# Layer 3 of a four-layer cross-attention kernel: hand order on four engines, exponentials after the pieces, value sums multiplied from PSUM

## The chip, the cores and the metric

The kernel runs on one core of a Trainium2 chip, in float32 throughout. The metric is the device time of one execution in microseconds; the time before is the median of three runs, 3840.64 us (3837.99 to 3846.04). A core has five instruction streams that matter here: TensorE (PE, with its weight loads as PEld), VectorE (DVE), ScalarE (ACT), GpSimd (POOL) and SyncE (SP), which issues the transfers. Each takes its own instructions in order, and waits for another only where a buffer or a value demands it.

## What is computed

Four layers follow each other on a tensor of 4 batches x 512 rows x 512 columns: a grouped-query attention (layer 0), two RWKV recurrences (layers 1 and 2), and a perceiver-style attention with an MLP (layer 3). Only layer 3 is touched:

```python
h = jnp.concatenate([x, latents], axis=1)             # x: context, latents: result of layer 2
q = (latents @ q_w + q_b).reshape(b, k_len, NH, DH)   # 16 heads of 32
kv = (h @ kv_w + kv_b).reshape(b, p + k_len, NH, DH, 2)
kmat, v = (kv[..., 0], kv[..., 1])
attn = jnp.einsum('bkhd,bnhd->bhkn', q, kmat) / DH    # 512 queries, 1024 keys
attn = softmax(where(full_mask, attn, -inf))
attn_out = jnp.einsum('bhkn,bnhd->bkhd', attn, v).reshape(b, k_len, H)
attn_out = attn_out @ out_w + out_b + residual
out = rmsnorm(attn_out, postnorm_w)
out = gelu(out @ mlp_w1 + mlp_b1) @ mlp_w2 + mlp_b2 + residual
```

## The kernel before, in words

Layer 3 splits its work into 16 **units**, a batch `b` times a slice `m` of 128 columns (4 heads of 32), numbered 0 to 15 here. The 1024 keys are 8 blocks of 128. A loop over **steps** (`for i in range(NU + NB + LAG)`, L1358) runs three units at once, each at a different stage, eight steps to a unit:

- `least(u, lt, a)` (L1179) for the newest unit: four score matmuls into `psc`, one for each head, and four VectorE operations (L1189) that keep the running minimum in `mx` (the scores are negated).
- `turned(old, s)` for the unit before: four transposed score matmuls into `pst` (L1175), four VectorE subtractions of the minimum `mb` (L1220) into the tile `aT`, then one ScalarE exponential over all 2048 columns (L1223 for the four masked context blocks, L1225 for the others), and on GpSimd a sum over the blocks into `acc` (L1228 once, L1230 six times). `spread` at s = 0 makes `mb` from `mx` (matmuls `pb`, ScalarE copies L1211).
- `values` two steps behind that (`LAG = 2`): four matmuls into `po` (L1235), which accumulates over eight blocks.

A unit closes in the step in which `ws` is 7, which is step s = 1 of the unit after it: `counted` (L1254) multiplies `acc` with ones into `pn` (L1235) and takes the reciprocal `rs` (L1261); `values` adds the last block and copies `po` into `y` on ScalarE (L1252); `divided` (L1263) multiplies `y` by `rs` (L1267).

Between these stand **pieces**, generators that yield after each bite of matmul work. `early` is the preparation of the next unit: `prep` makes `q`, keys (`pk`) and values (`pv`), and ahead of a new batch `begin` (L1113) loads context and mask (`mi` to `nm` L1121, `mci` to `mc` L1126) and transposes the residual (`ptx`). `rest` is the finish of the last complete batch: `finish` (L1269) multiplies by the output weights (`pout`), adds bias and residual (L1280, L1281), squares and sums on ScalarE (L1284), scales and takes the power -1/2 (`rms`, DVE L78, POOL L79), multiplies (L1286), adds `b2` to the residual on GpSimd (L1287), transposes (`ptn`, L1300), then runs the MLP: `ph` matmuls with a gelu eviction into `hT` (L1320), and `po` (here called `po2` after its code) with an addition into `x` (L1329). A step has a slot for a piece after `least` and one more after `turned`. `behind(i)` says how many of the 38 finish pieces should still be left at step i.

The pools matter: one PSUM pool of seven buffers (tag `s`) is handed round in order of allocation to `psc`, `pst`, `pb`, `pn` and the pieces; `po` has one buffer of its own; `aT` has three, `acc` and `mb` one each.

**What sets the order.** Layers 0 to 2 are inside `tc.manual_schedule` for PE, DVE, ACT and POOL: the instructions stand as written. Layer 3 is inside `tc.manual_schedule(engines={E.PE})`: TensorE's stand as written, and a scheduler decides those of the other engines (L1409).

```python
                if old:
                    turned(old, s)
                if left > min(34, behind(i)) and piece(rest):
                    left -= 1
                if 0 <= w < len(units):
                    values(units[w], ws)
                    if ws == NB - 1:
                        divided(units[w])
```

Of the kernel before, what the change touches and what calls it, by code (L numbers as in the profile page):

```python
# [8 lines left out]
F32 = mybir.dt.float32  # L9
I32 = mybir.dt.int32  # L10
AF = mybir.ActivationFunctionType
ALU = mybir.AluOpType
# [3 lines left out]
P = 128  # L16
B, L, C = 4, 512, 512
KC = C // P
# [12 lines left out]
def tile_xattn_rwkv_perceiver(ctx: ExitStack, tc: tile.TileContext, t: dict, out: bass.AP):  # L31
    nc = tc.nc
# [1054 lines left out]
    def layer3():  # L1087
        NH, HD, N = 16, 32, 2 * L
        NB = N // P
        NR = 4  # L1090
        T2 = 2 * P
        with (
# [18 lines left out]
            st = [{} for _ in range(B)]  # L1111
# [24 lines left out]
            def prep(b, m):  # L1136

                d = st[b]
                ms = slice(m * P, (m + 1) * P)
                w3 = {}  # L1140
                for x in "qkv":
                    w3[x] = bp.tile([P, KC, P], F32, tag="w3" + x, name="w3" + x)
                    nc.sync.dma_start(w3[x], t["L3_W" + x][:, ms].rearrange("(k p) n -> p k n", p=P))
                q = d["q", m] = bp.tile([P, L], F32, tag="q", name="q", bufs=3)
                pm = ps_s.tile([P, L], F32, tag="s", name="pq")
                mm(pm, [(w3["q"][:, k, :], d["xT"][:, k, :]) for k in range(KC)])
                nc.scalar.activation(q, pm, AF.Identity, bias=cols[:, m, 0:1], scale=-1.0 / HD)
                yield
                kT = d["k", m] = bp.tile([P, 2, L], F32, tag="kT", name="kT", bufs=3)
                v = d["v", m] = bp.tile([P, NB, P], F32, tag="v", name="v", bufs=3)  # L1150
                for a, src in enumerate((d["cT"], d["xT"])):
                    pm = ps_s.tile([P, L], F32, tag="s", name="pk")
                    mm(pm, [(w3["k"][:, k, :], src[:, k, :]) for k in range(KC)])
                    nc.scalar.activation(kT[:, a, :], pm, AF.Identity, bias=cols[:, m, 1:2])
                    yield
                    pm = ps_s.tile([P, LT, P], F32, tag="s", name="pv")
                    for j in range(LT):
                        mm(pm[:, j, :], [(src[:, k, j * P : (j + 1) * P], w3["v"][:, k, :]) for k in range(KC)])
                    nc.vector.tensor_tensor(
                        v[:, a * LT : (a + 1) * LT, :],  # L1160
                        pm,
                        vb[:, None, ms].to_broadcast([P, LT, P]),
                        ALU.add,
                    )
                    yield
# [3 lines left out]
            def row_scores(lhsT, rhs, name):  # L1169

                ps = []
                for r in range(NR):
                    rs = slice(32 * r, 32 * r + 32)
                    psc = ps_s.tile([P, L], F32, tag="s", name=name)
                    nc.tensor.matmul(psc, lhsT[rs], rhs[rs], start=True, stop=True, tile_position=(32 * r, 0))  # L1175
                    ps.append(psc)
                return ps
# [35 lines left out]
            def turned(u, s):  # L1213

                b, m = u
                d = st[b]
                ps = row_scores(d["k", m][:, s // LT, s % LT * P : (s % LT + 1) * P], d["q", m], "pst")
                w = d["w", s] = sp.tile([P, NR, L], F32, tag="aT", name="aT", bufs=3)
                for r in range(NR):
                    nc.vector.tensor_tensor(w[:, r, :], ps[r], d["mb"][:, r, :], ALU.subtract)  # L1220
                wf = w.rearrange("p r l -> p (r l)")
                if s < LT:
                    nc.scalar.activation(wf, wf, AF.Exp, bias=d["mc"][:, s : s + 1], scale=-1.0)  # L1223
                else:
                    nc.scalar.activation(wf, wf, AF.Exp, scale=-1.0)  # L1225
                if s == 1:
                    acc = d["acc", m] = sp.tile([P, NR, L], F32, tag="acc", name="acc", bufs=1)
                    nc.gpsimd.tensor_tensor(acc, d["w", 0], w, ALU.add)  # L1228
                elif s > 1:
                    nc.gpsimd.tensor_tensor(d["acc", m], d["acc", m], w, ALU.add)  # L1230

            def columns(po, lhsT, rhs, **kw):

                for r in range(NR):
                    nc.tensor.matmul(  # L1235
                        po[32 * r : 32 * r + 32, :], lhsT(r), rhs[:, r, :], tile_position=(0, 32 * r), **kw
                    )

            def values(u, s):

                b, m = u
                d = st[b]
                if s == 0:
                    d["po"] = ps_o.tile([P, L], F32, tag="o", name="po")
                v = d["v", m]
                columns(
                    d["po"], lambda r: v[:, s, 32 * r : 32 * r + 32], d["w", s], start=(s == 0), stop=(s == NB - 1)
                )
                if s == NB - 1:
                    if "y" not in d:  # L1250
                        d["y"] = bp.tile([P, KC, L], F32, tag="y", name="y")
                    nc.scalar.copy(d["y"][:, m, :], d["po"])  # L1252

            def counted(u):  # L1254

                b, m = u
                d = st[b]
                pn = ps_s.tile([P, L], F32, tag="s", name="pn")
                columns(pn, lambda r: ones, d["acc", m], start=True, stop=True)
                rs = d["rs", m] = sp.tile([P, L], F32, tag="sc", name="rs")  # L1260
                nc.vector.reciprocal(rs, pn)  # L1261

            def divided(u):  # L1263
                b, m = u
                d = st[b]
                y = d["y"][:, m, :]
                nc.vector.tensor_tensor(y, y, d["rs", m], ALU.mult)  # L1267

            def finish(b):  # L1269

# [63 lines left out]
            def chain(*gens):  # L1334
                for x in gens:
                    yield from x

            def piece(*gens):
                return any(next(x, NB) is None for x in gens)
# [4 lines left out]
            units = [(b, m) for b in range(B) for m in range(KC)]  # L1344
            NU = NB * len(units)

            def behind(i):

                if i < NU - NB * (KC - 1) + 2:
                    return 38 * ((1 - i) % (NB * KC)) // (NB * KC)  # L1350
                return sum(0.75 if j < NU - NB else 1.35 if j < NU else 2 for j in range(i + 1, NU + NB))
# [6 lines left out]
            for i in range(NU + NB + LAG):  # L1358
                n, s = divmod(i, NB)
                u, old = [units[j] if 0 <= j < len(units) else None for j in (n, n - 1)]  # L1360
                if u and s == 0:
                    for _ in early:
                        pass
                    b, m = u
                    if m + 1 < KC:
                        early = prep(b, m + 1)
                    elif b + 1 < B:
                        early = chain(begin(b + 1), prep(b + 1, 0))
                w, ws = divmod(i - NB - LAG, NB)
                if u and ws == 0 and w and w % KC == 0:  # L1370
                    for _ in rest:
                        pass
                    rest = finish(w // KC - 1)
                    left = 38
                if u:
                    least(u, s // 2, s % 2)
                if piece(early):
                    pass
                elif piece(rest):
                    left -= 1  # L1380
                if old:
                    if s == 0:
                        spread(old)
                if ws == NB - 1 and 0 <= w < len(units):
                    counted(units[w])
                if old:
                    turned(old, s)
                if left > min(34, behind(i)) and piece(rest):
                    left -= 1
                if 0 <= w < len(units):  # L1390
                    values(units[w], ws)
                    if ws == NB - 1:
                        divided(units[w])
# [5 lines left out]
    E = mybir.EngineType  # L1399
    with (  # L1400
# [5 lines left out]
        layer0(ahead, ep)  # L1406
        for _ in ahead:
            pass
    with tc.manual_schedule(engines={E.PE}):  # L1409
        layer3()  # L1410


# [62 lines left out]
```

## Time and profile before

| | |
|---|---|
| median of the three runs | 3840.64 us |
| profiled execution: its own time / its span | 3843.51 us / 3841.5 us |
| layers 0 to 2 | to about 2420 us of the span |
| layer 3, steps with full flow | about 2480 to 3700 us |
| layer 3, last finish | about 3700 us to the end |
| busy, share of the span: PE / DVE / ACT / POOL | 93% / 72% / 44% / 46% |
| granted TensorE clock, mean | 0.965 |

In the profile, times in a timeline row are the start in the span and the duration, both in us; in groups, busy us and mean ns of one. A bracket at a row's end is the idle time of its engine just ahead of it, with the instruction that ended it. An x8 row of `psc`, `pst`, `po` or `pn` is four matmuls (each has two records).

### The profile page before, as it was taken

How to read it: one execution, taken by the hardware profiler on the slowest of the kernel's cores; microseconds unless marked ns; L12 is line 12 of the kernel's file. 1: busy time of each engine (PE TensorE's matmuls, PEld its weight loads, DVE VectorE, ACT ScalarE, POOL GpSimd, SP SyncE). 2: the span in 40 equal slices, each digit the busy share in tenths (PEclk: the TensorE clock that was granted, in tenths of full speed). 3: DMA queues.
4: the chain of work that ended last, by engine and by line, in shares of the span. 5: the costliest groups of instructions: out<-in, count | busy, mean ns of one | idle time of the engine just before them, and what ended most of it. 6: DMA issues, size and time to landing. Idle time of an engine off the chain costs nothing.

```text
span 3841.5 us, 52407 instructions
## 1 busy us (share of the span) xinstructions
PE 3589.6 (93%) x20544; PEld 1900.9 (49%) x20544; DVE 2765.4 (72%) x4665; ACT 1691.6 (44%) x2514; POOL 1768.4 (46%) x834
## 2 busy tenths in 40 slices
PE   9999999988899999999999967899999999999989
PEld 3333333455565665655665634444454444544446
DVE  6777777689988888888888871388655665667531
ACT  4777676533444444444444422133343334324531
POOL 4777777424444444444444432065533433444430
PEclk9999999989999999999999988899999999999999
DMA  4000000166677777777777754200022122121223
GB/s 149 23 12 23 12 9 20 51 143 133 146 168 176 180 182 171 178 172 167 170 170 171 176 126 129 69 28 17 31 90 70 58 65 71 59 67 36 91 93 121
DMA packets 188805, 386.66 MB, mean 101 GB/s; under 512 B 18128, under 2 KB 44880, under 8 KB 186512
## 3 DMA queue, kind: packets, MB, share of 16 engines
q1 hardware_dynamic: 150256, 251.72, 20.8%
q0 software_dynamic: 38304, 131.61, 18.5%
q8 instruction: 162, 2.65, 0.3%
q14 instruction: 83, 0.68, 0.1%
HBM read 247.50 MB, written 4.19 MB: 66 GB/s over the span
## 4 chain that ended last, share of the span: by engine, by line
PE 64%; DVE 15%; DMA 6%; issue 5%; POOL 5%; ACT 5%; SPq 0%; POOLq 0%; DVEq 0%; ACTq 0%
PE pm L73 9%; PE pv L73 6%; PE po L73 5%; DMA kv<-A 5%; PE ph L73 5%; PE psc L242 5%; PE pst L279 4%; PE pst L1175 3%; PE psc L1175 3%; PE po L304 3%; PE pr L73 3%; DVE ry L867 3%; PE pk L73 3%; PE po L1235 2%; DVE kv L862 2%
## 5 line engine op out<-in xcount | busy, mean ns | idle before, releaser
L1230 POOL TENSOR_TENSOR acc<-acc,aT 128x2048 f32<-128x2048 f32 x96 | 435.0, 4531 | 420.4 <-ACT aT L1225 235.6
L292 POOL TENSOR_TENSOR aT<-aT,nmT 128x1536 f32<-128x1536 f32 x124 | 428.6, 3461 | 206.8 <-ACT aT L290 183.4
L254 DVE CUSTOM_DVE_ANT_0 sc<-psc,nm 128x512 f32<-128x512 f32 x512 | 354.0, 691 | 147.0 <-PE psc L242 89.3
L1220 DVE TENSOR_TENSOR aT<-pst,mb 128x512 f32<-128x512 f32 x512 | 317.4, 681 | 132.0 <-PE pst L1175 132.0
L867 DVE TENSOR_TENSOR ry<-kv,o_r 128x1024 f32<-128x1024 f32 x256 | 347.7, 1398 | 3.5
L862 DVE TENSOR_TENSOR_SCAN kv<-W,kv 128x1032 f32<-128x1032 f32 x128 | 296.1, 2313 | 0.2 <-DMA kv<-A 0.2
L584 POOL DMA_DIRECT2D kv<-A x127 | 118.9, 936 | 379.9 <-DVE kv L839 376.8
L290 ACT COPY aT<-pst 128x512 f32<-128x512 f32 x372 | 196.4, 595 | 178.2 <-PE pst L279 177.7
L298 ACT ACTIVATE aT<-aT 128x2048 f32<-128x2048 f32 x128 | 246.7, 1929 | 5.7 <-POOL aT L292 4.9
L73 PE MATMUL po<-l_m,hT 128*128 128x512 f32 x512 | 237.0, 606 | 9.2 <-ACT hT L1320 9.0
L73 PE MATMUL ph<-nT,l_m 128*128 128x256 f32 x1024 | 240.7, 391 | 0.0
L73 PEld LDWEIGHTS ph<-nT,l_m 128*128 128x128 f32 x1024 | 195.1, 194 | 64.9 <-issue 27.2
L1228 POOL TENSOR_TENSOR acc<-aT 128x2048 f32<-128x2048 f32 x16 | 72.4, 4524 | 327.6 <-ACT aT L1223 327.6
L833 DVE TENSOR_TENSOR A<-vr,o_k 128x1024 f32<-128x1024 f32 x128 | 155.6, 1216 | 88.1 <-DMA kv<-A 88.0
L279 PE MATMUL pst<-q,km 32*128 32x512 f32 x1024 | 206.2, 639 | 9.4 <-DVE mxs L254 5.8
L1189 DVE CUSTOM_DVE_ANT_0 sc<-psc,zeros,mx 128x512 f32<-128x512 f32 x256 | 177.5, 746 | 50.7 <-PE psc L1175 48.4
L1225 ACT ACTIVATE aT<-aT 128x2048 f32<-128x2048 f32 x64 | 122.3, 1911 | 196.6 <-DVE aT L1220 191.6
L1223 ACT ACTIVATE aT<-aT,mc 128x2048 f32<-128x2048 f32 x64 | 128.2, 2003 | 180.3 <-DVE aT L1220 171.0
L242 PE MATMUL psc<-km,q 32*128 32x512 f32 x1024 | 198.8, 653 | 0.8 <-ACT q L223 0.8
L881 PE MATMUL py<-ry,k 128*32 128x512 f32 x1024 | 158.5, 626 | 42.4 <-DVE ry L867 29.6
L929 POOL TENSOR_TENSOR gn_rs<-gn_rs,mhalf 128x64 f32<-128x64 f32 x16 | 186.4, 11648 | 23.0 <-DVE gn_rs L927 23.0
L1189 DVE CUSTOM_DVE_ANT_0 sc<-psc,nm 128x512 f32<-128x512 f32 x256 | 162.9, 686 | 46.5 <-PE psc L1175 45.0
(266 smaller groups left out, 7189.9 us busy)
## 6 DMA issues: line engine op xcount, KB each, us to landing
l_m<-in_L_W SPq DMA_DIRECT2D x64, 1024.0 KB, 5.1
kv<-A POOLq DMA_DIRECT2D x127, 516.0 KB, 7.4
L_wk<-in_L_Wk SPq DMA_DIRECT2D x16, 1024.0 KB, 8.0
L_wr<-in_L_Wr SPq DMA_DIRECT2D x16, 1024.0 KB, 7.8
L_wv<-in_L_Wv SPq DMA_DIRECT2D x16, 1024.0 KB, 6.0
L_wg<-in_L_Wg SPq DMA_DIRECT2D x16, 1024.0 KB, 7.8
L_wo<-in_L_Wo SPq DMA_DIRECT2D x64, 256.0 KB, 7.5
L_fk<-in_L_fWk SPq DMA_DIRECT2D x16, 1024.0 KB, 8.3
```

The lines of the kernel that those rows point to most:

```text
L73: nc.tensor.matmul(ps, lhsT, rhs, start=(i == 0), stop=(i == len(pairs) - 1))
L242: nc.tensor.matmul(psc, d["q"][g][rs, lt * P : (lt + 1) * P], d["km"][rs, a, :], start=True, stop=True, tile_position=(32 * r, 0),)
L254: nc.vector.tensor_tensor_reduce(sc, ps[r], d["nm"][lt], 1.0, -3.0e38, ALU.add, ALU.max, mxs[:, a, lt, c : c + 1])
L279: nc.tensor.matmul(pst, d["km"][rs, a, s * P : (s + 1) * P], d["q2", a][rs, :], start=True, stop=True, tile_position=(32 * r, 0),)
L292: nc.gpsimd.tensor_tensor(w[:, n:, :], w[:, n:, :], nmT[:, None, :].to_broadcast([P, NR - n, L]), ALU.add)
L298: nc.scalar.activation(w, w, AF.Exp)
L862: nc.vector.tensor_tensor_scan(flat(kv), flat(W[g % 2]), flat(kv), 0.0, ALU.mult, ALU.add)
L867: nc.vector.tensor_tensor(y, kv[:, 4 * h : 4 * h + 4, None, :TP].to_broadcast([P, 4, 2, TP]), d["r"][:, i].rearrange("p (o m) -> p o m", o ...
L1175: nc.tensor.matmul(psc, lhsT[rs], rhs[rs], start=True, stop=True, tile_position=(32 * r, 0))
L1189: nc.vector.tensor_tensor_reduce(sc, ps[r], d["nm"][a], 1.0, mx[:, 0, lt, r : r + 1] if a else 3.0e38, ALU.add, ALU.min, mx[:, a, lt, r : ...
L1220: nc.vector.tensor_tensor(w[:, r, :], ps[r], d["mb"][:, r, :], ALU.subtract)
L1230: nc.gpsimd.tensor_tensor(d["acc", m], d["acc", m], w, ALU.add)
```

## The change

Four things, all in layer 3:

1. The whole of layer 3 is in `manual_schedule` for all four engines, so DVE, ACT and POOL too take their instructions as written.
2. The exponential and the sum into `acc` leave `turned` and become `weights(old, s)`, called after the second piece slot.
3. The reciprocal leaves `counted` and becomes `inverted`, called after `turned`; the matmuls into `pn` stay where they are.
4. ScalarE's copy of `po` is gone; `divided` multiplies `po` in PSUM by `rs` into `y`.

```diff
-                if s == NB - 1:
-                    if "y" not in d:
-                        d["y"] = bp.tile([P, KC, L], F32, tag="y", name="y")
-                    nc.scalar.copy(d["y"][:, m, :], d["po"])
...
+            def inverted(u):
+                d = st[u[0]]
+                rs = d["rs"] = sp.tile([P, L], F32, tag="sc", name="rs")
+                nc.vector.reciprocal(rs, d["pn"])
...
             def divided(u):
                 b, m = u
                 d = st[b]
-                y = d["y"][:, m, :]
-                nc.vector.tensor_tensor(y, y, d["rs", m], ALU.mult)
+                if "y" not in d:
+                    d["y"] = bp.tile([P, KC, L], F32, tag="y", name="y")
+                nc.vector.tensor_tensor(d["y"][:, m, :], d["po"], d["rs"], ALU.mult)
...
                 if old:
                     turned(old, s)
+                if ws == NB - 1 and 0 <= w < len(units):
+                    inverted(units[w])
                 if left > min(34, behind(i)) and piece(rest):
                     left -= 1
+                if old:
+                    weights(old, s)
...
-    with tc.manual_schedule(engines={E.PE}):
+    with tc.manual_schedule(engines={E.PE, E.DVE, E.Activation, E.Pool}):
         layer3()
```

Set side by side, the built orders of the two kernels differ in this and in nothing else:

- TensorE: not at all. Layers 0 to 2: not at all.
- VectorE: the reciprocal (16 times) stands after the four subtractions instead of ahead of them, and `y` right behind it, or behind one `x` addition. In each `finish` the scale of `rms` and the multiplication of `ao` stand right behind the addition of the residual; before, one minimum lay ahead of the first and another between the two. `mc` stands beside `nm` instead of up to a unit ahead.
- ScalarE: the 16 copies of `po` are gone. Gelu evictions and squares stand ahead of the exponential of their step instead of behind it. The table loads between gelu and exponential fall from 86 to 74 in the program.
- GpSimd: the power of `rms` stands ahead of that step's sum into `acc` and of the addition of `b2`; before, both lay ahead of it.
- SyncE: three loads of `mci` stand behind their batch's `mi` instead of at the start of the layer.

More of the change, by code (lines that the diff above doesn't have):

```diff
@@ L1220, in turned, with weights @@
                     nc.vector.tensor_tensor(w[:, r, :], ps[r], d["mb"][:, r, :], ALU.subtract)
+            def weights(u, s):
+                b, m = u
+                d = st[b]
+                w = d["w", s]
                 wf = w.rearrange("p r l -> p (r l)")
@@ L1257, in counted @@
                 d = st[b]
-                pn = ps_s.tile([P, L], F32, tag="s", name="pn")
+                pn = d["pn"] = ps_s.tile([P, L], F32, tag="s", name="pn")
                 columns(pn, lambda r: ones, d["acc", m], start=True, stop=True)
-                rs = d["rs", m] = sp.tile([P, L], F32, tag="sc", name="rs")
-                nc.vector.reciprocal(rs, pn)
+            def inverted(u):
+                d = st[u[0]]
+                rs = d["rs"] = sp.tile([P, L], F32, tag="sc", name="rs")
+                nc.vector.reciprocal(rs, d["pn"])
             def divided(u):
```

## The prediction

> **What bounds the kernel now.** First the table of windows, layer 3 by stretch (us; busy of PE, PEld, DVE, ACT, POOL with counts; granted clock; DMA): steps of batch 0, its finish up to the transposes, the long flow after, the last unit.
>
> ```profile
> 2546.00:2710.00 164.00, 162.27 (x932) 72.29 (x928) 137.03 (x303) 62.66 (x52) 95.29 (x21) 1.00 0.08 23
> 2710.00:2770.00 60.00, 52.31 (x259) 25.46 (x256) 41.81 (x92) 14.10 (x16) 29.80 (x13) 0.97 0.09 27
> 2770.00:3060.00 290.00, 285.95 (x1435) 141.36 (x1433) 178.05 (x361) 119.19 (x120) 108.68 (x24) 0.99 0.22 72
> 3610.00:3703.00 93.00, 80.14 (x341) 37.98 (x339) 34.26 (x43) 44.01 (x45) 34.91 (x8) 0.96 0.29 96
> ```
>
> TensorE is busy nearly throughout, so only its stops count: 7.7 us in the finish, 12.9 in the last unit. What ends them say the waits of PE from 2480 us on (us, times, longest):
>
> ```profile
> PE pout L73 <- DVE mx L1189: 11.2, 6, 3.2
> PE po L73 <- ACT hT L1320: 9.0, 7, 5.0
> PE ptn L1296 <- DVE mx L1189: 5.4, 2, 2.7
> PE pn L1235 <- POOL acc L1230: 5.1, 1, 5.1
> PE pst L1175 <- DVE mx L1189: 4.3, 2, 2.3
> PE psc L1175 <- DVE rs L1261: 1.4, 4, 0.4
> ```
>
> A stop costs more than its idle time. In PE's timeline, `pout` after a stop of 3.18 us takes 5.40 instead of 3.70; the granted clock over 3077 to 3081 is 0.57:
>
> ```profile
> 3077.16 5.40 PE L73 MATMUL pout<-l_wo,y 128*128 128x512 f32 x8 [3.18 <-DVE mx L1189]
> ...
> 3090.62 3.70 PE L73 MATMUL pout<-l_wo,y 128*128 128x512 f32 x8 [0.41 <-DVE mx L1189]
> ```
>
> So I count from start to start, less what the group takes undisturbed: `pst`, `psc` 1.07, `pout`, `pk` 3.63, `ph` 3.65. The clock's share after a stop is then 1.7.
>
> **Gain 1: the power in the finish, 16.6.** The timeline of batch 0's first finish step:
>
> ```profile
> 2723.17 4.65 POOL L1230 TENSOR_TENSOR acc<-acc,aT 128x2048 f32<-128x2048 f32 x1 [2.26 <-ACT aT L1223]
> ...
> 2727.79 1.26 POOL L1287 TENSOR_TENSOR x<-x,b 128x512 f32<-128x512 f32 x1
> ...
> 2729.01 0.57 POOL L79 TENSOR_TENSOR rms<-rms,mhalf 128x1 f32<-128x1 f32 x1
> ...
> 2729.61 0.49 DVE L1286 TENSOR_SCALAR ao<-ao,rms 128x512 f32<-128x512 f32 x1 [4.04 <-POOL rms L79]
> ```
>
> The power waits behind the sum and the addition; DVE sits 4 us with two minima behind it, PSUM fills, TensorE stops. Afterwards the power stands first. The chain square 0.8, scale 0.15, power 0.55 with handovers is 1.6 us, and DVE waits through it. DVE's step is then 2.7 minima + 1.4 additions + 1.6 + 0.45 + 2.4 subtractions + 0.6 = 9.2, beside 10.5 on TensorE (1.07 + 3.63 + 1.07 + 3.63 + 1.0): hidden. So `pst` to `pout` shrinks to 1.07: in batch 0 from 3.21 and 3.23 (4.3 us); batch 1 gives 3.25 + 1.7 + 1.2, batch 2 3.25 + 1.7 + 1.1. At the fourth `pout` I count nothing: the sum into `acc`, now later, meets the addition of `x` (two SBUF inputs), and such a meeting at 3083.32 took 4.16 instead of 0.69. DVE stays late at `ptn`, for another reason.
>
> **Gain 2: `y` from PSUM, 20.7.** The tiles' rows (ns min/median/max):
>
> ```profile
> L1267 DVE TENSOR_TENSOR y<-y,rs x16: 675/1624/4707, 2549.9 to 3705.4; 128x512 f32<-128x512 f32 x16
> ```
>
> `y` comes out between 0.68 and 4.7 us, long wherever the sum runs on POOL. Subtraction L1220, with one PSUM input, is 621 to 694 ns over all 512, so 0.69 for the new `y`. The long ones cost TensorE: unit 5, `pst` at 2894.28 takes 5.07 (+4.0) and `ph` 5.34 (+1.7); unit 9, at 3241.39, 4.7 + 2.2; units 6 and 10, `psc` at 2988.48 and 3336.73 takes 3.45 (+2.4), `pk` +1.7. In the other units nothing waits for it. ScalarE's 16 copies (9.3 us) were off the path, as ScalarE is idle half the time.
>
> **Gain 3: gelu ahead of the exponential, 6.9 in the flow and 10.7 at the end.** Three `pst` pairs (2820.11, 3167.21, 3503.46) take 2.40 because gelu frees PSUM late, 3 x 1.33; `pb` waits 2 x 0.9; `po2` 2 x 0.5. In the last unit `po2` waits 0.35 + 4.98 + 1.34 + 1.13 for the second gelu, which stands behind exponential and table load; the new gelu ends 0.9 after `ph`, needed 2.8 after. With 1.6 of clock that is 9.4, and the last exponential loses its table load ahead of `pn`: 1.3.
> The exponential itself comes up to 6 us later (`ph` 3.7, gelu 0.84, load 1.28). Queued behind it is the sum of 4.5; its readers `po` come two steps later, 19 us or more. Cover gone, it would cost up to 6 a step. The 12 table loads less (15 us) are ScalarE's own.
>
> **Loss: `pn` is held longer, 28.0.** The timeline of unit 0's close:
>
> ```profile
> 2544.18 1.14 PE L1175 MATMUL pst<-q,kT 32*128 32x512 f32 x8
> 2544.31 3.36 DVE L1261 RECIPROCAL rs<-pn 128x512 f32<-128x512 f32 x1 [1.48 <-PE pn L1235]
> ...
> 2547.59 2.42 DVE L1220 TENSOR_TENSOR aT<-pst,mb 128x512 f32<-128x512 f32 x4
> 2547.73 1.66 PE L1175 MATMUL psc<-kT,q 32*128 32x512 f32 x4 [0.36 <-DVE rs L1261]
> ```
>
> Seven buffers go round: `pn`, four `pst`, two `psc`; the third `psc` needs `pn` back. The reciprocal freed it at 2547.7. Now the subtractions go first: they start 1.23 after `pst`, as at 2554.32, 2545.4 to 2547.8, then the reciprocal to 2551.1. TensorE resumes 3.4 later, though the fourth `psc` no longer waits for its `pst`: the group ends at 2552.2 instead of 2549.3, +2.9. Behind DVE's reciprocal are `y` and four minima, which fit beside the next `pv` of 3.77. TensorE now idles 3.9, so the clock drops: +1.7. The same at units 2, 3 and 13, which show the 0.36: 4 x 4.6 = 18.4. Unit 1, where DVE is behind anyway: 2.0. With a `ph` of 3.65 between (units 4, 6, 8, 10, 12) the reciprocal ends 1.25 after the second `psc` is due: 6.3. Units 5 and 9: 0.4 each. Units 7 and 11 have 9 us of pieces there; 14 and 15 no `psc`.
> `mc` now waits for its own load, queued on SP behind `mi`: landing 4.6 (median) beside 3.5 for `mi`, 0.4 issued later, so 1.5 on DVE with the subtractions behind it. Bounds 0 and 3.2 (6.7 against 3.5); 0.5 in batch 0, where DVE is late; in the other two 1.36 of DVE's idle time covers it.
>
> [...]
>
> **Sum.** 16.6 + 20.7 + 17.6 = 54.9 against 28.0: -27. The profiled execution took 3843.5, of which the span is 3841.5: 3816.5, and as the runs' median lies 2.9 lower, 3814 is predicted.
>
> **Rivals.**
> - *The reciprocal's stops win (slower).* Mechanism: `pn` held behind DVE's subtractions, and DVE not catching up, so that all 12 units with a `psc` soon after pay the full stop, 3.9 + 1.7: 67 against 54.9, +12, 3853. A unit pays where TensorE has under 6.9 us of work (2544.2 to 2551.1) from `pst` to the `psc` that wants `pn`; the sign turns at 4.6 a unit. For it: four units pay so already. Against: a `ph` in that place gives 3.65 of cover in five, a `po2` in two.
> - *Given back (no change).* The finish hands its stops on to `ptn` and the MLP, gain 1 gone, and half of gain 2 turns into waits for subtractions: 54.9 - 16.6 - 10.3 = 28, against 28: 3841. The same time follows if the order does not do what it says; the moved instructions in the built order speak against that.
> [...]
>
> **Chances.** Likeliest 0.50, lighter 0.18, no change 0.12, slower 0.20. A measurement of this kernel tells about 0.2% (7.7 us) from no change; so faster 0.68, same 0.12, slower 0.20. The range, 3797 to 3847, takes in the lighter case and, beyond no change, the upper bound of `mc` (3.2 in each of three batches) up to half way to the slower case.
>
> **What would show it.** Right: power ends its waits in the first three finish steps below 2 us and no `pst` to `pout` gap there; `y` at 0.69 throughout; no `po` wait on `hT` in the last unit; the wait of `psc` on `rs` grown from 1.4 to about 25 us (4 x 3.8, unit 1 2.6, 5 x 1.25, 2 x 0.4). Wrong: stops on `aT` or `acc` in the flow, which would mean late exponentials; `psc` waits in units 4 to 12 over 3 us; new waits at `ptn` longer than the old ones.

## The result, and the profile after

The changed kernel took 3797.55 us (median of 3795.7 to 3798.82) beside 3843.34 for the kernel before on the same chip: a ratio of 0.988, 95% interval 0.986 to 0.990. Carried to the 3840.64 of before that is 3793, under the low end of the forecast's range. The direction was right and the size too small: 27 us were forecast, 46 to 47 came.

The profiled execution took 3798.02 us, its span 3796.2. The instructions of TensorE are in the same order in both kernels, so the starts of its groups can be laid side by side, and each change of the difference put down to a place. That is the ledger used below. The spans themselves must be split first: in the fourteen profiles of this study layer 3 (from its first `pq`) begins between 2409.5 and 2429.4 us, although nothing ahead of it differs. I therefore compare "layer 3": the span less that start. Before it is 1416.0, after 1369.5: 46.5 less. There is one profile of each kernel, so how far layer 3's own span varies from one execution to the next was not measured; a difference of a few us counts here only where the ledger finds it at one place.

TensorE's idle time in layer 3 by what ended it, from the waits of PE in the changed kernel, 2480 to 3800 us (us, times, longest):

```profile
PE psc L1175 <- DVE aT L1220: 11.6, 4, 4.2
PE ptn L1302 <- DVE ao L1292: 6.6, 2, 4.1
PE pn L1241 <- POOL acc L1236: 3.8, 1, 3.8
```

The waits of `pout`, `pst` and `po` are gone from this list. So is the wait of `psc` on `rs`, which was to grow from 1.4 to about 25. New are long waits of `psc` on the subtractions; before there was one, of 0.9. The finish and the last unit of the changed kernel, at the places of those two windows of before:

```profile
2712.32:2769.63 57.31, 54.15 (x260) 26.99 (x256) 47.93 (x92) 14.38 (x16) 30.27 (x13) 0.94 0.09 28
3575.03:3656.10 81.07, 77.28 (x341) 37.89 (x339) 29.98 (x43) 33.28 (x36) 35.01 (x8) 0.98 0.33 111
```

The finish is 2.7 us shorter than its 60, and of 7.7 us of idle PE 3.2 are left; the last unit is 11.9 shorter than its 93, and of 12.9 idle 3.8 are left.

Unit 0's close in the changed kernel's timeline, the rows that were to show the loss:

```profile
2544.21 1.14 PE L1175 MATMUL pst<-q,kT 32*128 32x512 f32 x8
...
2545.44 2.48 DVE L1220 TENSOR_TENSOR aT<-pst,mb 128x512 f32<-128x512 f32 x4 [2.57 <-PE pst L1175]
2546.28 1.63 PE L1175 MATMUL psc<-kT,q 32*128 32x512 f32 x8
...
2547.84 3.35 DVE L1266 RECIPROCAL rs<-pn 128x512 f32<-128x512 f32 x1
```

The reciprocal starts where the forecast had it, 3.5 us later than before. But all four `psc` are over at 2547.9, just as it starts: none of them can have waited for `pn`'s buffer. Part of the delay comes back a step later. The `pst` behind the next `pv`, before and in the changed kernel:

```profile
2553.09 1.14 PE L1175 MATMUL pst<-q,kT 32*128 32x512 f32 x8
```

```profile
2551.60 2.77 PE L1175 MATMUL pst<-q,kT 32*128 32x512 f32 x8
```

Its third and fourth matmuls go into the banks of the first two `psc`, and the minima that free these now stand behind the later reciprocal. So the `psc` end 1.5 us earlier than before, and this `pst` loses 1.6.

The ledger against the steps of the forecast:

| step | forecast, us | ledger, us |
|---|---|---|
| gain 1, finish | -16.6 | -11.9 (about -3.1, -4.6, -4.1 by batch) |
| gain 2, `y` from PSUM | -20.7 | -20.7 |
| gain 3, gelu in the flow | -6.9 | -7.6 |
| gain 3, at the end | -10.7 | about -10 |
| loss, `pn` held longer | +28.0 | +5.5 |

The five lines come to 44.7 of the 46.5; the rest lies at places that no step names. At the end 11.1 are gained in the last unit and 1.3 lost again in the last finish.

### The profile page after: what moved, and what is told of

It reads as the page before. It is cut to its first block, busy times and chain, and to the rows that moved or that the text cites. A ratio compares the mean times of both kernels' runs of the same rounds, so it can differ in the third digit from the quotient of the medians.

```text
span 3796.2 us, 52369 instructions
## 1 busy us (share of the span) xinstructions
PE 3570.5 (94%) x20544; PEld 1900.4 (50%) x20544; DVE 2759.9 (73%) x4665; ACT 1668.2 (44%) x2486; POOL 1771.0 (47%) x834
## 4 chain that ended last, share of the span: by engine, by line
PE 71%; DVE 13%; DMA 6%; issue 4%; POOL 3%; ACT 2%; SPq 0%; DVEq 0%; POOLq 0%; ACTq 0%
PE pm L73 9%; PE ph L73 6%; PE pv L73 6%; PE po L73 6%; DMA kv<-A 5%; PE psc L242 5%; PE pst L279 4%; PE pst L1175 4%; PE psc L1175 4%; PE pr L73 3%; PE pk L73 3%; PE po L304 3%; PE po L1241 3%; DVE ry L867 3%; DVE kv L862 2%
```

## Where `pn`'s buffer goes: the experiments on the reciprocal

Theory: buffers are handed out in the order in which their last readers stand in the program. Moving the reciprocal behind the four subtractions then moves `pn`'s buffer behind the four of `pst`, and so away from the third `psc`. Rival, the forecast's: `pn`'s place in the ring is fixed, and the stops are somewhere else in the trace. The built programs say which bank each tile has; unit 0's close, without `po`:

```
before   pn:3 pst:1 pst:2 pst:0 pst:6 psc:5 psc:4 psc:3 psc:1 pv:2 pst:0 pst:6
changed  pn:3 pst:1 pst:2 pst:0 pst:6 psc:5 psc:4 psc:1 psc:2 pv:0 pst:6 pst:3
```

Before, bank 3 goes to the third `psc`; in the changed kernel to the second `pst` of the next step, four tiles later. So the pool is not handed round in the order of allocation, as the description of the kernel before has it: in the second row `pn` comes round behind its four `pst`. The same shift of four is found in every unit but the last (12 units give it to `psc` before; the expectation below says 13). Two runs put times to it.

**Reciprocal first.** `inverted` is called right behind `counted`; the rest is the changed kernel.

```diff
                     counted(units[w])
+                    inverted(units[w])
...
-                if ws == NB - 1 and 0 <= w < len(units):
-                    inverted(units[w])
```

> The changed kernel with one move undone: the reciprocal stands ahead of the four subtractions again. In the built order of PSUM banks the bank of `pn` then goes to the third `psc` of the next step in 13 of 16 units, as before the change; in the changed kernel it goes, four tiles later, to the second `pst` of the step after that. Theory of the prediction (holding `pn` cost 28.0 in the changed kernel): the whole loss comes back, 3797.5 - 28 = 3770. Theory of release order (banks are handed out in the order in which their last readers stand in the program, so moving the reciprocal moved the bank's next user too, and the trace shows only 5.5 lost): 3797.5 - 5.5 = 3792, with psc's wait on rs back at 0.36 in units 0 to 3 and 13.

Measured: 3793.4 us (0.988 of before, interval 0.986 to 0.989); layer 3 is 1367.0, 2.5 less than in the changed kernel. `psc` waits for `rs` again, 1.6 in all. So by the profiles the move of the reciprocal costs 2.5 us; by the totals, each beside its own before, the two kernels can't be told apart. Either way it is not 28.

**`pn` third, and late.** Four one-column reads of the `pst` tiles behind the reciprocal bring back the bank order of before while the reciprocal stays late: the forecast's premise, built. They take 0.29 us together.

```diff
+                d["ps"] = ps
...
                     inverted(units[w])
+                    if old:
+                        end = sp.tile([P, NR], F32, tag="end", name="end")
+                        for r in range(NR):
+                            nc.vector.tensor_copy(end[:, r : r + 1], st[old[0]]["ps"][r][:, 0:1])
```

> The changed kernel with four one-column copies on DVE behind the reciprocal, one from each `pst`. They make the reciprocal release `pn` ahead of the four `pst` in program order, so that the third `psc` gets the bank of `pn`, while the reciprocal stays behind the subtractions: the premise of the prediction, built. Theory of release order with the prediction's prices: a wait of psc on rs of about 3.8 in units 0, 2, 3 and 13, 1.25 in five units with a `ph` between, and the sum 28.0 in place of the 5.5: 3797.5 + 22.5 = 3820, plus 16 times some 0.4 on DVE where it is late. Rival (such stops are made up behind, so the price itself was wrong): within 8 of the changed kernel, 3798 to 3805, with psc waits on rs under 1 us.

Measured: 3824.3 us (0.995, 0.994 to 0.997); layer 3 is 1404.0, 37.0 more than with the reciprocal first. Its waits of PE, and unit 0's close in its timeline:

```profile
PE psc L1175 <- DVE end L1400: 20.9, 10, 3.9
```

```profile
2545.13 3.35 DVE L1267 RECIPROCAL rs<-pn 128x512 f32<-128x512 f32 x1
...
2548.63 1.55 PE L1175 MATMUL psc<-kT,q 32*128 32x512 f32 x4 [3.93 <-DVE end L1400]
...
2550.11 5.02 PE L73 MATMUL pv<-w3v,cT 128*128 128x128 f32 x32
```

Here is the stop that the changed kernel lacks: the group of `psc` splits, the second half waits 3.93 for the reciprocal (the row names the reads right behind it), and `pv` behind it takes 5.02 in place of 3.84 (clock 0.75 there, 1.00 in the changed kernel). By the ledger from the run above to this one, units 0, 2, 3 and 13 lose 4.6, 5.3, 4.6 and 6.3, where 4.6 each was priced; the five with a `ph` between lose 1.4 to 1.7, priced at 1.25; units 5 and 9 0.5, priced at 0.4; unit 1 loses 6.5, priced at 2.0. The price was about right. What it was put on did not exist in the changed kernel.

## `y` from PSUM: undone, and alone

**The copy put back** into the changed kernel: ScalarE copies `po`, VectorE multiplies SBUF by SBUF.

```diff
+                if s == NB - 1:
...
+                    nc.scalar.copy(d["y"][:, m, :], d["po"])
...
-                nc.vector.tensor_tensor(d["y"][:, m, :], d["po"], d["rs"], ALU.mult)
+                y = d["y"][:, m, :]
+                nc.vector.tensor_tensor(y, y, d["rs"], ALU.mult)
```

> The changed kernel with part four undone: ScalarE copies `po` to `y` in SBUF, and VectorE multiplies SBUF by SBUF. Theory: 20.7 come back, because the multiplication is again 1.6 us in the middle and up to 4.7 where the sum runs on GpSimd: 3797.5 + 20.7 = 3818. Rival: in the new order the multiplication meets the sum at other times, and waits for the copy behind the exponential; if it no longer meets it, y stays below 1 us and the time within 5: 3800.

Measured: 3859.0 us (1.004, 1.003 to 1.006); layer 3 1439.1, 69.6 more than the changed kernel and 23 more than before. Neither theory had the size. Its tile row of `y` (ns min/median/max), under it that of the changed kernel:

```profile
L1276 DVE TENSOR_TENSOR y<-y,rs x16: 693/3931/4972, 2543.0 to 3719.3; 128x512 f32<-128x512 f32 x16
```

```profile
L1273 DVE TENSOR_TENSOR y<-po,rs x16: 677/692/693, 2551.3 to 3658.7; 128x512 f32<-128x512 f32 x16
```

The median is 3.9 us where it was 1.6 before the change. The new order starts the reciprocal when the exponential starts, so the product comes just as GpSimd begins its sum; the timeline of unit 0 in this run:

```profile
2542.20 4.49 POOL L1234 TENSOR_TENSOR acc<-aT 128x2048 f32<-128x2048 f32 x1 [12.04 <-ACT aT L1229]
2543.02 4.21 DVE L1276 TENSOR_TENSOR y<-y,rs 128x512 f32<-128x512 f32 x1
...
2547.90 2.24 PE L1175 MATMUL pst<-q,kT 32*128 32x512 f32 x4 [3.44 <-DVE mx L1189]
```

The product ends half a microsecond after the sum, four minima stand behind it, and TensorE stops for 3.44; ten such waits make 32.4 us. So the order makes this part necessary.

**Part four alone**, in the kernel before. ScalarE's order loses the copies and is otherwise the same; on VectorE the scheduler also moves the product of units 4, 6, 8, 10 and 12 ahead of minima that it stood behind.

```diff
-                    nc.scalar.copy(d["y"][:, m, :], d["po"])
...
-                nc.vector.tensor_tensor(y, y, d["rs", m], ALU.mult)
+                nc.vector.tensor_tensor(d["y"][:, m, :], d["po"], d["rs", m], ALU.mult)
```

> The kernel before with part four alone: `y` is the product of `po` in PSUM and the reciprocal, ScalarE's copies go; the order of the other instructions is left to the scheduler as before. Theory of the prediction (part four is worth 20.7 by itself): 0.9946 of the kernel before, some 3820. Rival (the scheduler places the product elsewhere once the copy is gone, or another wait takes its place): within 5 of before.

Measured: 3808.7 us (0.991, 0.989 to 0.993); layer 3 1392.7, 23.3 less than before. In the ledger the eight terms of gain 2 are there to 0.1 us and sum to 20.7. Besides, the three `pst` pairs give their 1.33 each, and the last unit 5.3, where the longest wait of `po` on gelu falls from 5.0 to 1.2: both had been put down to gelu's new place. But gelu still stands behind the exponential in this run. VectorE in the last unit, before and here:

```profile
3632.03 4.71 DVE L1267 TENSOR_TENSOR y<-y,rs 128x512 f32<-128x512 f32 x1 [3.28 <-ACT y L1252]
3636.66 2.47 DVE L1220 TENSOR_TENSOR aT<-pst,mb 128x512 f32<-128x512 f32 x4
```

```profile
3603.15 0.68 DVE L1264 TENSOR_TENSOR y<-po,rs 128x512 f32<-128x512 f32 x1
3607.38 2.48 DVE L1220 TENSOR_TENSOR aT<-pst,mb 128x512 f32<-128x512 f32 x4 [3.55 <-PE pst L1175]
```

Before, the product waited for ScalarE's copy, which stood behind the exponential, and so it began together with the sum and took 4.71. The subtractions behind it came late, and with them the next exponential and the gelu that TensorE waited for. Here the subtractions wait for their `pst` alone. Ahead of the first `pst` pair it is the same with a product of 2.56. Other places lose 6.7 of the gain again.

## Exponential, sum and power

**The order alone**: the kernel before with only `manual_schedule` for four engines.

> The kernel before, with part one of the change alone: the order of the code on all four engines in layer 3, nothing moved in the code. The power then stands ahead of GpSimd's addition and sum. Exponential stays ahead of the second piece's evictions (so the finish's square waits up to 1.9 for it), `y` stays a product of two SBUF tiles, the reciprocal stays first. Theory (each part gives its share by itself): the finish gains about 12 less the square's waits of 5 to 10, the rest is as before: 3841.5 - 5 = 3836. Rival (the order alone puts the sum right beside the product of `y`, as in the run that undid part four, where its median was 3.93 us): slower than before by 15 to 40, 3856 to 3880, with a median of `y` above 3 us.

Measured: 3920.1 us (1.022, 1.020 to 1.024); layer 3 1498.5, 82.5 more than before; the median of `y` is 4.69. The rival was right in kind, with twice the upper end of its size. The longest of this run's waits of PE:

```profile
PE pst L1175 <- DVE mx L1189: 46.7, 19, 4.0
```

By the ledger 31 of the 82.5 are lost at the closes of units 0 to 3 alone, ahead of any finish, where the product stands ahead of the minima. A premise of mine was wrong too: in the code as it was written the sum stands ahead of the finish's power, so that following the code keeps the power behind it. Taken by itself, part one does harm; only part two, which takes exponential and sum out of `turned`, puts the power first.

**Exponential and sum early** in the changed kernel: `weights` called ahead of the second piece.

```diff
+                if old:
+                    weights(old, s)
                 if left > min(34, behind(i)) and piece(rest):
                     left -= 1
-                if old:
-                    weights(old, s)
```

> The changed kernel with the exponential called straight behind the subtractions (and the reciprocal), ahead of the second piece's evictions. Theory: the gains of gelu come back as losses, 7.6 in the flow and 10 at the end, and in the finish the square now waits up to 1.9 for an exponential in each of 12 steps, which puts some 5 to 10 more on TensorE: 3797.5 + 17.6 + 5 = 3820. Rival (the gelu waits were covered, and the last unit's 10 came from the sum): 3797.5 + 5 = 3803.

Measured: 3832.9 us (0.998, 0.997 to 0.999); layer 3 1415.2, 45.7 more than the changed kernel. 38 of it lies in the three finishes. The first finish step in this run's timeline:

```profile
2709.11 4.51 POOL L1236 TENSOR_TENSOR acc<-acc,aT 128x2048 f32<-128x2048 f32 x1 [4.96 <-ACT aT L1229]
...
2709.71 0.15 DVE L78 TENSOR_SCALAR rms<-ss 128x1 f32<-128x1 f32 x1 [0.79 <-ACT sq L1290]
...
2713.58 0.57 POOL L79 TENSOR_TENSOR rms<-rms,mhalf 128x1 f32<-128x1 f32 x1
```

The power's input is there at 2709.86; the power starts at 2713.58, when the sum ends. The square is hardly late. That speaks against my reason (the square behind the exponential) and for the sum ahead of the power, and two runs part them.

**Early except in the finish's first steps** (`late = left > 32` keeps `weights` behind the piece there).

> The changed kernel with the exponential early again (behind the subtractions) except in the first steps of each finish, where it stays behind the piece with the square. Theory (the run with all exponentials early lost 38 of its layer-3 loss of 45 us in the finish, where VectorE waits for the square behind the exponential; gelu itself accounts for the rest): 7 to 10 slower than the changed kernel, ratio to before about 0.990. Rival (gelu is worth the 17.6 of the prediction): ratio 0.9923.

Measured: 3799.0 us (0.988, 0.985 to 0.990), which the total can't tell from the changed kernel; layer 3 1375.7, 6.2 more. Some 7 are lost in the last unit and 1 in the flow; 2 come back elsewhere.

**Exponential early, sum late**: `weights` cut in two, with the sum called behind the piece.

> The changed kernel with the exponential early again, behind the subtractions, but GpSimd's sum left where the change put it, behind the second piece. Theory (in the run with both early, the finish lost 38 because the sum stood ahead of the power again): the power waits for nothing here, only the square can stand behind an exponential of 1.9 to 2.0; layer 3 about 6 to 10 slower than in the changed kernel for gelu, and 0 to 10 for the square: about 1380, against 1415 with both early; ratio to before 0.990. Rival (the square behind the exponential is what cost the finish its 38): layer 3 near 1415, ratio 0.998.

Measured: 3800.8 us (0.991, 0.989 to 0.993); layer 3 1379.7, as the theory said; 6.3 of the 10.2 is again in the last unit. So what part two gives the finish, it gives by keeping the sum behind the power: with both early 38 us are lost there, with the exponential alone under 3.

## The finish's own size

Where did 4.7 of the 16.6 go? The first finish step of the changed kernel:

```profile
2726.91 0.57 POOL L79 TENSOR_TENSOR rms<-rms,mhalf 128x1 f32<-128x1 f32 x1 [5.80 <-DVE rms L78]
2727.46 1.26 POOL L1293 TENSOR_TENSOR x<-x,b 128x512 f32<-128x512 f32 x1
2727.51 1.50 DVE L1292 TENSOR_SCALAR ao<-ao,rms 128x512 f32<-128x512 f32 x1 [0.68 <-POOL rms L79]
```

The power is at once followed by GpSimd's addition of `b2`, which starts 0.05 ahead of the multiplication; that takes 1.50, priced at 0.45 after the 0.49 of before. All 16 are so. And the fourth step, where the forecast counted nothing:

```profile
2753.67 1.63 DVE L1287 TENSOR_TENSOR ao<-ao,x 128x512 f32<-128x512 f32 x1
...
2756.96 1.48 DVE L1292 TENSOR_SCALAR ao<-ao,rms 128x512 f32<-128x512 f32 x1 [0.66 <-POOL rms L79]
2758.36 2.47 DVE L1220 TENSOR_TENSOR aT<-pst,mb 128x512 f32<-128x512 f32 x4
2759.09 3.27 PE L1175 MATMUL psc<-kT,q 32*128 32x512 f32 x6 [3.16 <-DVE aT L1220]
```

VectorE is late by the delays of four steps, the subtractions come late, and TensorE stops for 3.16; from 2760 to 2764 its granted clock is 0.50. Three runs take the delays away one by one.

**`b2` later**: the addition leaves the four steps for the two of the transposes.

```diff
-                    nc.gpsimd.tensor_tensor(x, x, b2, ALU.add)
...
                     nTs.append(nT)
+                    for x in xn[b][2 * h : 2 * h + 2]:
+                        nc.gpsimd.tensor_tensor(x, x, b2, ALU.add)
```

> The changed kernel with GpSimd's addition of the bias b2 to x moved from right behind the power to the transposes' steps. Theory: this addition starts 0.06 us ahead of VectorE's multiplication by the power and holds it up, 1.49 us in place of the 0.49 it took before the change; with the two apart it takes 0.49, VectorE is 2.0 us earlier by the subtractions of the fourth step, the stop of psc on aT there falls from 3.2 to some 1.2, and three batches give 2 to 3 each, the end 1: 3797.5 - 8.5 = 3789. Rival (the multiplication is long for another reason, or the subtractions' place is set by PE): multiplication still above 1 us, or time within 2 of the changed kernel.

Measured: 3784.6 us (0.987, 0.985 to 0.989); layer 3 1362.4, 7.1 less than the changed kernel. The multiplication:

```profile
L1292 DVE TENSOR_SCALAR ao<-ao,rms x16: 485/488/1477, 2726.1 to 3668.4; 128x512 f32<-128x512 f32 x16
```

The median is back at 0.49, so its neighbour was the cause. But only about 3 of the gain is at the end and 2.5 in the three finishes: the longest wait of `psc` on the subtractions is still 3.3. In the fourth step VectorE's own addition of `x` now takes 2.38, where it took 1.63, and at its longest the multiplication still takes 1.48 (the 1477).

**One addition from PSUM**: as that, and `ob` added to `x` by GpSimd during the unit before, so that `ao` is one sum of `pout` and `x`; `b2 - ob` is added later.

```diff
-                    nc.vector.tensor_tensor(ao, pm, ob, ALU.add)
-                    nc.vector.tensor_tensor(ao, ao, x, ALU.add)
+                    nc.vector.tensor_tensor(ao, pm, x, ALU.add)
...
```

> The run before this (b2 added later) and the output bias added to x ahead of time by GpSimd, so that VectorE has one addition from PSUM per finish step and not two; b2 less the output bias is added at the end, so that the sum stays what it was. Theory: the fourth step loses the 0.69 of the third and the 1.63 of its own second addition, the stop of psc there goes, and the chain to ptn shortens by 0.7 to 1.6: another 2 to 3 for each of three batches and about 1 at the end, 3789 - 8 = 3781. Rival (VectorE has slack by then and the stop has another cause; or GpSimd's four more additions delay the sum): no better than the run before, 3789 to 3795.

Measured: 3773.7 us (0.983, 0.982 to 0.985); layer 3 1351.2, 18.3 less than the changed kernel. The waits of `psc` on the subtractions are 3.6, where the changed kernel had 11.6. Around the second finish the granted clock is 0.97 (3056 to 3105 us), where the changed kernel had 0.93 (3060 to 3110). How much of the gain is the stops and how much the clock behind them was not separated.

**`b2` later still**, ahead of the first `po2`:

> The fastest kernel so far (one addition from PSUM per finish step, b2 added in the transposes' steps) with b2's additions moved on again, to right ahead of the first products that need them. Theory: the multiplication of the fourth step, which still took 1.48 us beside such an addition, falls to 0.49, so VectorE's subtractions there come 1.0 earlier and the last ptn wait of 3.0 falls by 1.0: three times 1.0 to 1.5 and 1.0, 4 to 5 less than that kernel, ratio to before 0.982. Rival (the remaining 1.0 stops are the subtractions' own): the same as that kernel, 0.9834.

Measured: 3774.0 us (0.982, 0.980 to 0.983); layer 3 1349.6, 1.6 less than the last; by its total not to be told from it. Its waits of PE:

```profile
PE pn L1242 <- POOL acc L1237: 3.8, 1, 3.8
PE ptn L1301 <- DVE ao L1292: 3.0, 1, 3.0
PE psc L1176 <- DVE aT L1221: 1.9, 2, 1.0
```

The `psc` stops are nearly gone, but the `ptn` wait did not fall by 1.0. The end of this run's timeline shows why:

```profile
3653.61 0.55 POOL L79 TENSOR_TENSOR rms<-rms,mhalf 128x1 f32<-128x1 f32 x1 [2.88 <-DVE rms L78]
3654.13 5.12 POOL L1331 TENSOR_TENSOR x<-x,b 128x512 f32<-128x512 f32 x4
3654.20 1.48 DVE L1292 TENSOR_SCALAR ao<-ao,rms 128x512 f32<-128x512 f32 x1 [0.73 <-POOL rms L79]
```

In the last finish no sum stands between the power and the additions of `b2`, so GpSimd starts them right behind the last power however late they stand in the code, and the last multiplication still takes 1.48. These two kernels beat both of the case, by 1.7 to 1.8% of before.

**That with the reciprocal first**:

> The last kernel with the reciprocal ahead of the subtractions as well. Theory (the two are in different places, unit closes and finish, and add up): 4 below the last, 3777. Rival (they share VectorE's lateness): no better than the last.

Measured: 3783.9 us (0.986, 0.984 to 0.988); layer 3 1360.0, 8.8 more than without. It doesn't add up, and I can't say that the reciprocal's place is why. The ledger puts about 4 of it behind the finish of batch 0, where the order of TensorE and the stops (0.85 and 0.86) are the same in both. This run's timeline, then that of the run without:

```profile
2761.04 3.69 PE L1176 MATMUL pst<-q,kT 32*128 32x512 f32 x8
2764.66 6.64 PE L73 MATMUL ph<-nT,l_m 128*128 128x256 f32 x16
```

```profile
2759.42 2.48 PE L1176 MATMUL pst<-q,kT 32*128 32x512 f32 x8
2761.83 3.72 PE L73 MATMUL ph<-nT,l_m 128*128 128x256 f32 x16
```

`ph` takes 6.64 at a granted clock of 0.55 (2764.66 to 2771.24) and 3.72 at 1.00 (2761.83 to 2765.48), so the clock accounts for at least part of the 8.8. Why it is low under `ph` in one kernel and not in the other stays open.

## Why the prediction was wrong, by its own steps

- **The step that failed** is the loss of 28.0, and in it the sentence "Seven buffers go round: `pn`, four `pst`, two `psc`; the third `psc` needs `pn` back". It took the ring of before, where `psc` waited 0.36 for `rs`, for a property of the kernel. It was a result of the reciprocal's place: the pool gives buffers out in the order of their last readers, and with the reciprocal `pn`'s turn moved back behind the four `pst`. Its next user then comes in the next step, when it is free. The bank table shows the order, the run with `pn` third shows the stop wherever the premise holds, and its sizes there were close to the forecast's: 37.0 in all for 27.5, nearly half of the excess in unit 1. In the changed kernel the loss is 2.5 by the run with the reciprocal first, 5.5 by the ledger from before, and what is left of it is largely the next `pst` waiting for minima, as in unit 0. With it, the forecast's own sum would have been 54.9 - 5.5 = 49 for the 46.5 measured.
- **Gain 1**, 16.6 for 11.9: the mechanism held (the power no longer stands behind the sum and the addition, `pst` to `pout` is undisturbed in the first steps). Two terms were mis-sized: the multiplication, 0.45 counted and 1.49 measured, and the fourth step, nothing counted and +6.0, +5.7 and +2.7 in the three batches up to the second `ptn`. The first is a meeting with GpSimd: its addition runs from 2727.46 to 2728.72, the multiplication from 2727.51 to 2729.01, and with the addition moved the median is 0.49 again. Why this operation, with one input in SBUF, is held up and the subtractions, with one in PSUM, are not (mean 0.68 before and after), no run here shows. I had reckoned with such meetings only for operations on two SBUF tiles.
- **Gain 2**, 20.7, was right in each of its eight terms, in the change and alone. Two sentences beside them were wrong. "In the other units nothing waits for it": the product also held up the three `pst` pairs and the last unit, 4.0 and 5.3. And ScalarE's copies were not off the path, as the product waited for them and so met the sum. That the parts don't simply add was not seen either: in the new order the old product would have cost 69.6.
- **Gain 3** was right in sum (about 17.6) partly by luck, as its cause was not gelu's place alone: those 4.0 and 5.3 come with part four and nothing else, and putting the exponential back early took only 6 to 10 from the gain in layer 3.
- **Rivals.** "Reciprocal's stops win" needed 4.6 in each of 12 units; where the stops were built they cost 3.0 on average, and layer 3 stayed 12 below before. The lighter case in the chances and in the range rests on a term for the clock that no run shows; in the runs the stops were absent from the changed kernel, the longest one built, 3.93, was followed by a clock of 0.75, and the end of the finish grew.
- **The clock after a stop**, counted at 1.7, had nothing to act on in the changed kernel's closes that were to stop. Where the stop was built, 3.93 long, `pv` behind it ran at 0.75 and took 5.02 in place of 3.84. Before, the stops of 2.28 in unit 5 and 2.00 in unit 9 were followed by a granted clock of 0.77 (2897.7 to 2905 us) and 0.50 (3245 to 3251), though the stops of 2.06 and 2.09 were followed by 1.00 (2730.8 to 2734.6, 2743.5 to 2747.3). So the length of a stop alone does not decide it.
- **Signs.** Three of the four for right came: VectorE's 16 waits for the power were 10.8 us in all, `y` stayed at 0.69, and no `po` waited on `hT` in the last unit. The fourth, the grown wait on `rs`, did not. Of those for wrong, stops on `aT` came, but from late subtractions and not from late exponentials, and the longest wait of `ptn` grew from 3.6 to 4.1.

## What to carry to other kernels

When a reader moves in a program, ask not only when its buffer comes free but who gets that buffer next: where the pool goes by the order of the last readers, the answer moves with the reader, and a trace of before shows only the old pairing. Read the buffer assignment of the changed program before a wait for one buffer is priced. And price parts of a change in the order that they will run in: the explicit order alone cost 82 us here, and 46 were gained only because the sum was moved behind the power and the product taken out of SBUF. Moving an instruction down in the code delays it only where its engine has something to do in between, as GpSimd's additions at the end show.

## What the runs showed of the hardware

- A VectorE multiplication by a per-partition scalar, with one SBUF input, goes from 0.49 to 1.49 us beside a GpSimd addition of 1.26, and ends 0.3 after it; a product of two SBUF tiles goes from 0.69 to 4.97 beside a sum of 4.5. The 512 subtractions with one input in PSUM kept their mean of 0.68.
- Behind the same order of TensorE and the same short stop (0.85 and 0.86 us) `ph` took 6.64 us at a granted clock of 0.55 in one profile and 3.72 at 1.00 in another.
- The part of the program ahead of layer 3, the same in all kernels, took 2409.5 to 2429.4 us: more than most single effects here, which is why they are read from layer 3's own span.
